# A four-layer graph network on one core: the order of the first loads, and what the planner believes of chains and of the wire

## The chip, the cores and the metric

The kernel runs on one core of a Trainium2 chip. The metric is the time of one execution on the device, in microseconds; several runs are taken, and the median is given. Five engines matter: PE (TensorE, matmuls), with PEld for its weight loads; DVE (VectorE); ACT (ScalarE); POOL (GpSimd); and SP (SyncE), which issues most of the DMAs. DMAs can also be issued from ACT and POOL.

## What is computed

32 graphs of 512 nodes with 256 features each, x of shape (32, 512, 256), and an adjacency of 512 x 512 whole numbers for every graph. Four layers follow each other, each with its own kind of attention, and each adds its result to x. All is in float32.

```python
h = relu(layernorm(x))                                 # before every layer
# layer 0
q = h @ att_W;  s = softmax(q @ h.T / 16 + where(adj == 1, 0, -1000))
y = h
for W, b in ((W0, b0), (W1, b1)):  y = tanh(s @ (y @ W + b))
x = x + y
# layer 1
Wh = h @ W.T;  e = leaky(Wh @ a1 + (Wh @ a2).T)
x = x + softmax(where(adj > 0, e, -9e15)) @ Wh
# layer 2
Hh = h @ W;    e = where(adj != 0, exp(-leaky(Hh @ a_src + (Hh @ a_dst).T)), 0)
x = x + elu((e @ Hh) / rowsum(e))
# layer 3
hW = h @ W
e = leaky((hW @ a_1).T + hW @ a_2 + hW @ a_12 @ hW.T)
p = softmax(where(adj > 0, e, -9e15))
x = x + elu(h @ W_1 + (p @ h) @ W_2)
```

## The kernel before

**Tiles.** The 512 nodes of a graph are four tiles of 128 (NT), the 256 features two halves of 128 (HC). Most products are made in two halves each way with seven products in place of eight (the helper `seven`, with sums of halves on DVE from `block_sums`); graph 0's layer 0, and the attention of layers 0, 1 and 2 in every graph and of layer 3 in the last five, are made plainly. PSUM's 8 banks, 34 pages of SBUF and a few smaller buffers are pools.

**A plan for the whole program.** No loop runs at the time of execution. Every piece of work of all 32 graphs is first noted as an operation: its engine (PE, V for DVE, A for ACT, G for POOL, D for SP's DMAs, L for a landing that no engine carries out), its cost as a pair (how long it holds the engine, when its result is there), the operations that it comes after, the buffers that it uses, and for a DMA its size in bytes. `Plan.order` then runs through time as a list scheduler: whenever an engine is free, it takes the ready operation that is due first, where the due times are counted backwards from a start time for each graph. `Plan.replay` goes through such an order and gives the time that the planner believes it will take. `Plan.best` tries start times (regular distances of 32 to 62 us and four last distances, then single graphs moved by 8, 4 and 2 us) and keeps the order that `replay` finds shortest. The kernel emits the instructions in this order; each engine then runs its own in that sequence and waits on semaphores where a result or a buffer isn't there yet. So a belief of the planner changes no instruction, but it changes the sequence on every engine, which buffer each takes, and how graphs overlap.

**What the planner believes of time.** In `order`, an operation that comes after another is ready PASS = 200 ns after the other's result, also when both are on the same engine; in `replay` it is HOP = 100 ns. A PE operation's cost has 170 ns between holding the engine and the result, so in `order` the next step of a chain on PE is ready 370 ns after PE is free of the step before. Chains on PE are: the four steps of `attend` (L794 to 796), the four of the second convolution's first product (L1049), and the four transposes of `turn` (L772). All DMAs share one wire, RATE = 200 bytes per ns, and land LAND = 2000 ns after their last byte (and 800 ns more in `order`). `SLACK` lengthens DVE's and ACT's costs by 3% in `order`.

**Before the plan's order** the constants are set, and ACT issues the load of b0 (L456), which only the values of layer 0 read (L960 for graph 0, L983 for the others).

**The start within the plan.** ACT issues two early loads (L461): layer 3's W (`l3_here`) and a12 (`a12_here`), then an activation that brings the table of functions in (`warm`, L483). W is turned on PE (L396), copied by ACT (L384), and multiplied with a12 and with itself (L414) into the matrix m3 that layer 3 needs. SP issues the four tiles of graph 0's x (L531), the weights w0 and att of layer 0 (L453), the four adjacency tiles of graph 0 (L534), and so on; in the planner w0 and att come after graph 0's x, and graph 0's adjacency after w0 and att. Graph 1's x comes after nothing. The other weights are loaded by POOL (L362), after graph 0's adjacency. A graph's x is one load of 512 KB, graph 0's is four of 128 KB. A graph's adjacency is four loads of 256 KB.

**Work of a graph that is named later.** L590 to L603: statistics, root, offset and normed rows of a layer (DVE, POOL, DVE, ACT). L608, L611, L623: the rows split in two planes of 16 bits, turned by a DMA transpose and joined again into hT. L552, L555: the adjacency as a code of 16 bits, and turned (by PE for graph 0, L559). L907: features for layers 0 and 3 (bank_f0p, bank_f3p). L933: values (bank_v, bank_w). L998 and L1166: scores of layers 0 and 3. L756, L761: a row of layers 1 and 2 sent to all partitions by way of DRAM. L791: `attend`. L868: the same by seven products, layer 3 of the first 27 graphs. L1042, L1060: second convolution of layer 0. L1247 to L1290: the end of layer 3 and the store.

Of the kernel before, what the change touches and what calls it, by code (L numbers as in the profile page):

```python
# [15 lines left out]
AF = mybir.ActivationFunctionType  # L16
# [40 lines left out]
class Plan:  # L57
# [9 lines left out]

    APART, APART_LAST = [1000.0 * k for k in range(32, 64, 2)], [1000.0 * k for k in (2, 5, 8, 12)]
    STEPS = [8000.0, 4000.0, 2000.0]
    HOP = 100.0  # L70
    LAND, RATE = 2000.0, 200.0
    SLACK = {"V": (1.03, 0.0), "A": (1.03, 0.0), "G": (1.5, 0.0), "D": (1.0, 800.0)}

    def __init__(self):
# [2 lines left out]
    def op(self, engine, cost, after, emit, graph, uses=(), size=0):  # L77


        much, more = self.SLACK.get(engine, (1.0, 0.0))  # L80
        plain, cost = cost, (cost[0] * much, cost[1] * much + more)
        flat = []
        for a in after:
            flat += a if isinstance(a, tuple) else [a]
        o = {"engine": engine, "cost": cost, "after": [a for a in flat if a is not None], "emit": emit,
             "graph": graph, "uses": list(uses), "number": len(self.ops), "size": size, "late": more, "plain": plain}
        self.ops.append(o)
        return o

# [38 lines left out]
    def replay(self, order):  # L128

        if len(order) < len(self.ops):  # L130
            return float("inf")
        at, end, owners, before, wire = {}, {}, {}, {}, 0.0
        for o in order:
            start = max([at.get(o["engine"], 0.0)] + [end[a["number"]] + self.HOP for a in o["after"]])
            for p in o["uses"]:
                where = p["pool"], p["number"]
                owner = owners.get(where)
                if owner is None or owner[0] is not p:
                    before[where] = owner[1] if owner else []
                    owner = owners[where] = p, []  # L140
                waits = before[where]
                if p["pool"] == "bank":
                    waits = waits + [x for x in owner[1] if x["engine"] != o["engine"]]
                start = max([start] + [end[x["number"]] + self.HOP for x in waits])
                owner[1].append(o)
            holds, until = o["plain"]
            if o["size"]:
                wire = max(wire, start) + o["size"] / self.RATE
                until = wire - start + self.LAND
            at[o["engine"]], end[o["number"]] = start + holds, start + until  # L150
        return max(end.values())

    def order(self, pools, starts):
        free = {pool: list(range(n)) for pool, n in pools.items()}
        users = {}
# [26 lines left out]
        while True:  # L182
            for e in engines:
                skipped = []
                while at[e] <= now and ready[e]:
# [8 lines left out]
                        p["number"] = free[p["pool"]].pop(0)  # L194
                    holds, until = o["cost"]
                    if o["size"]:
                        wire = max(wire, now) + o["size"] / self.RATE
                        until = wire - now + self.LAND + o["late"]
                    at[e] = now + holds
                    for p in o["uses"]:  # L200
                        p["ends"][e] = now + until + self.PASS
                    out.append(o)
                    heapq.heappush(events, (at[e], next(numbers), None))
                    heapq.heappush(events, (now + until + self.PASS, next(numbers), o))
                for x in skipped:
                    heapq.heappush(ready[e], x)
            if not events:
                break
            now = events[0][0]
            while events and events[0][0] <= now:  # L210
                o = heapq.heappop(events)[2]
                if o is None:
                    continue
                for p in o["uses"]:
                    p["users"] -= 1
                    if not p["users"]:
                        free[p["pool"]].append(p["number"])
                for w in users.get(o["number"], []):
                    w["left"] -= 1
                    if not w["left"]:  # L220
                        heapq.heappush(ready[w["engine"]], (w["rank"], w))
# [4 lines left out]
def kernel(  # L226
# [225 lines left out]
    for n, dst, w, key in (("w0", w0_s, w0, "raw9"), ("att", att_s, att_w, "raw10")):  # L452
        ready[key] = [prepare("D", D_X, [], lambda w=w, key=key: nc.sync.dma_start(  # L453
            out=raw(key)(), in_=rows_of(w)), key, size=P * HC * H * 4)]
        ready[n] = seven_of(raw(key), dst, HALF, ready[key], key)
    nc.scalar.dma_start(out=b0_sb, in_=line_of(b0))  # L456
    warm = const.tile([P, 1], F32, tag="warm", name="warm")

    def early(dst, src, key):
# [20 lines left out]
    ready["l2"] = seven_of(l2_wide, l2_aug, HALF + 1, a, "raw12")  # L480

    l3_here, a12_here = early(l3_sb, rows_of(l3_w), "raw2"), early(a12_sb, rows_of(l3_a12), "raw3")
    prepare("A", A_WARM, [l3_here[0], a12_here[0]], lambda: nc.scalar.activation(warm, zero, AF.Exp))  # L483
    t = transposed(l3_sb, wt3, [l3_here[1]], "raw2", "raw4", by="A")
    a = product(lambda d: awt()[:, d, :], a12_sb, lambda c: wt3()[:, c, :], H,
                t + [a12_here[1]], "raw3", "raw4", "raw5", by="A")
# [21 lines left out]
    def graph(b, adj_before, x_before, codes_before):  # L508
# [24 lines left out]
        def fetch_adj(t):  # L533
# [2 lines left out]

        got_x = [op("D", D_X, [x_before, codes_before], partial(fetch_x, ts), "x", "ahead", size=P * H * 4 * (ts.stop - ts.start))
                 for ts in ([slice(t, t + 1) for t in range(NT)] if b == 0 else [slice(0, NT)])]
        got_adj = [adj_before]
        for t in range(NT):  # L540

            got_adj.append(op("D", D_ADJ, got_adj[-1:] if b else [], partial(fetch_adj, t), "adj", size=P * N * 4))
        if b == 0:
            for n in ("raw9", "raw10"):
                ready[n][0]["after"] += got_x[-1:]
            for o in got_adj[1:]:
                o["after"] += ready["raw9"] + ready["raw10"]
            for o in loads:
                o["after"] += got_adj[-1:]

        def classes(g):
            nc.vector.tensor_scalar(T["code"][:, two(g), :], T["adj"][:, two(g), :], HUGE, None, ALU.mult)  # L552
# [740 lines left out]
            op("G", G_STORE, last, store, "y3", "slot", "ahead", size=N * H * 4)  # L1293
        return code, got_x[-1]

    codes, got_x = [None, None], [None, None]
    for b in range(B):
        code, got = graph(b, codes[-1], got_x[-2], codes[-2])
        codes.append(code)
# [38 lines left out]
```

## Time and profile before

| what | value |
|---|---|
| median of 3 runs | 2325.57 us (2325.55 to 2326.66) |
| the profiled execution | 2327.81 us, its span 2326.0 us |
| instructions | 38151 |
| first matmul / last matmul ends | 7.24 us / about 2320.2 us |
| DMA packets | 430243, 178.30 MB |
| granted clock of TensorE, mean | 0.999 |

The page has the busy time of each engine, the span in 40 slices, the chain of work that ended last, and the costliest groups of instructions. PE is where the chain runs: it has 92% of it, ACT 3%, DVE 2%, DMA 1%. The largest group on it:

```profile
L791 PE MATMUL bank_a<-v,e 128*128 128x258 f32 (+2 forms) x3232 | 817.2, 381 | 1.3 <-DVE e L1080 0.6
```

A line of this kind gives the source line, engine, operation, what is written from what, shapes and count, then the busy time in us and the mean of one in ns, then the idle time of the engine ahead of it and what ended most of that. Matmuls overlap in these records (a mean of 381 ns, while they start some 217 ns apart), so the distance from one start to the next tells more than the length of one.

### The profile page before, as it was taken

Reading aid. Unit: us, or ns where it says so; the run is one execution under the profiler, and the core shown is the slowest. Engines: PE = TensorE matmul, PEld = TensorE weight load, DVE = VectorE, ACT = ScalarE, POOL = GpSimd, SP = SyncE. Lnnn points to the kernel's source line nnn. Section 1 sums busy time; section 2 is a strip of 40 time slices with the busy share of each in tenths; the row PEclk is TensorE's granted clock in tenths of the full one; section 3 lists DMA queues with packets and bytes.
Section 4 is the critical chain, followed back from the end, with each engine's and each line's share of the span. In section 5 each row is a group of like instructions: output and inputs, shape, how many; then the busy total and the mean of one; then the engine's idle time right before and its main releaser. Section 6 shows DMA issues by size and latency. Waiting matters only on the chain.

```text
span 2326.0 us, 38151 instructions
## 1 busy us (share of the span) xinstructions
PE 2307.2 (99%) x13022; PEld 1996.3 (86%) x13022; DVE 2113.0 (91%) x5310; ACT 1720.1 (74%) x3279; POOL 257.5 (11%) x341
## 2 busy tenths in 40 slices
PE   8999999999999999999999999999999999999998
PEld 6888888888888888888888888988888888888887
DVE  6888889999999999999999999999999999998998
ACT  4677778767787777787777877778867778666884
POOL 2101101110101010100101011101111011010110
PEclk9999999999999999999999999999999999999999
DMA  6441233423333323333233333233332333321221
GB/s 163 114 96 37 60 78 78 91 61 74 89 73 87 73 69 87 87 73 82 66 79 87 76 87 70 70 88 83 75 82 63 87 82 73 92 54 25 61 50 45
DMA packets 430243, 178.30 MB, mean 77 GB/s; under 512 B 384128, under 2 KB 402176, under 8 KB 430048
## 3 DMA queue, kind: packets, MB, share of 16 engines
q1 hardware_dynamic: 424288, 157.51, 31.3%
q0 software_dynamic: 5072, 17.70, 2.3%
q8 instruction: 102, 1.67, 0.3%
q14 instruction: 93, 0.76, 0.1%
q10 hardware_dynamic: 688, 0.66, 0.1%
HBM read 67.64 MB, written 16.89 MB: 36 GB/s over the span
## 4 chain that ended last, share of the span: by engine, by line
PE 92%; ACT 3%; DVE 2%; DMA 1%; issue 0%; SPq 0%; ACTq 0%; DVEq 0%
PE bank_a L791 28%; PE bank_z L1042 8%; PE bank_s3p L1166 5%; PE bank_q0p L998 5%; PE bank_o L1060 4%; PE bank_v0p L933 4%; PE bank_f0p L907 4%; PE bank_w3p L933 4%; PE bank_f3p L907 4%; PE bank_a3p L868 4%; PE bank_s3q L1166 3%; PE bank_q0q L998 3%; PE bank_a3q L868 3%; PE bank_v1p L933 2%; PE bank_v2p L933 2%; PE bank_v3p L933 2%
## 5 line engine op out<-in xcount | busy, mean ns | idle before, releaser
L791 PE MATMUL bank_a<-v,e 128*128 128x258 f32 (+2 forms) x3232 | 817.2, 381 | 1.3 <-DVE e L1080 0.6
L791 PEld LDWEIGHTS bank_a<-v,e 128*128 128x128 f32 x3232 | 576.4, 190 | 70.6 <-issue 5.2
L603 ACT ACTIVATE xn<-x,off,rstd 128x256 f32<-128x256 f32 x512 | 278.2, 598 | 203.0 <-DVE off L599 197.6
L596 POOL TENSOR_TENSOR rstd<-ve,mhalf 128x2 f32<-128x2 f32 x256 | 222.4, 899 | 1737.6 <-DVE ve L593 1537.6
L623 ACT COPY hT<-planesT 128x512 uint16<-128x512 uint16 x508 | 375.9, 771 | 47.4 <-DMA planesT<-planes 47.0
L1042 PE MATMUL bank_z<-e,y 128*128 128x512 f32 x512 | 240.5, 593 | 0.0
L590 DVE BATCH_NORM_STATS2 st<-x 128x6 f32<-128x512 f32 x256 | 177.3, 698 | 9.3 <-DMA x<-in_x_dram 8.0
L608 DVE COPY planes<-xn 128x512 uint16<-128x512 uint16 x380 | 155.4, 419 | 13.6 <-DMA planesT<-planes 8.2
L765 ACT ACTIVATE e<-row,v 128x512 f32<-128x512 f32 x224 | 154.7, 727 | 5.2 <-DMA row<-row 5.2
L1042 PEld LDWEIGHTS bank_z<-e,y 128*128 128x128 f32 x512 | 90.6, 191 | 64.4 <-issue 59.5
L768 ACT ACTIVATE e<-e 128x1024 f32<-128x1024 f32 x128 | 136.8, 1069 | 0.1
L1060 PE MATMUL bank_o<-w_sb,zT 128*128 128x256 f32 x512 | 117.4, 379 | 0.0
L1173 DVE SCALAR_TENSOR_TENSOR e<-bank_s3p,v,mask 128x256 f32<-128x256 f32 x256 | 111.4, 477 | 3.7 <-PE bank_s3p L1166 3.2
L1006 ACT ACTIVATE e<-e 128x512 f32<-128x512 f32 x124 | 77.9, 634 | 43.6 <-DVE e L1017 41.8
L1060 PEld LDWEIGHTS bank_o<-w_sb,zT 128*128 128x128 f32 x512 | 96.9, 190 | 13.0
L697 DVE TENSOR_TENSOR hs<-hT,hs 128x256 f32<-128x256 f32 x254 | 105.9, 417 | 0.4
L728 ACT COPY v<-bank_v2p 128x258 f32<-128x258 f32 x128 | 48.2, 377 | 70.1 <-PE bank_v2p L933 69.0
L700 DVE TENSOR_TENSOR hs<-hT 128x512 f32<-128x512 f32 x127 | 86.9, 684 | 11.7 <-ACT hT L623 11.3
L1080 DVE SCALAR_TENSOR_TENSOR e<-codeT,e 128x1024 f32<-128x1024 bf16 x64 | 78.0, 1219 | 12.5 <-ACT e L768 12.4
L1009 DVE TENSOR_TENSOR e<-bank_q0p,mask 128x512 f32<-128x512 f32 x124 | 84.8, 684 | 4.0 <-PE bank_q0p L998 3.4
L1261 ACT ACTIVATE r<-y,one 128x512 f32<-128x512 f32 (+1 forms) x65 | 46.5, 715 | 50.8 <-DVE y L1271 42.8
L1111 DVE SCALAR_TENSOR_TENSOR e<-codeT,e 128x1024 f32<-128x1024 bf16 x64 | 77.9, 1218 | 6.6 <-ACT e L768 6.5
(224 smaller groups left out, 5386.9 us busy)
## 6 DMA issues: line engine op xcount, KB each, us to landing
adj<-in_adj_dram SPq DMA_DIRECT2D x128, 256.0 KB
x<-in_x_dram SPq DMA_DIRECT2D x31, 512.0 KB
out_dram<-y POOLq DMA_DIRECT2D x31, 512.0 KB, 3.4
row<-row SPq DMA_DIRECT2D x56, 256.0 KB
planesT<-planes SPq DMA_TRANSPOSE x508
codeT<-code SPq DMA_TRANSPOSE x124
crest<-crest SPq DMA_TRANSPOSE x64
row<-sT SPq DMA_DIRECT2D x56, 2.0 KB
```

The lines of the kernel that those rows point to most:

```text
L590: nc.vector.bn_stats(T[f"st{l}"][:, g, :], T["x"][:, two(g), :].rearrange("p t h -> p h t"))
L596: nc.gpsimd.tensor_tensor(T[f"rstd{l}"][:, two(g)], T[f"ve{l}"][:, two(g)], mhalf[:, two(g)], ALU.pow)
L603: nc.scalar.activation(T[f"xn{l}"][:, t, :], T["x"][:, t, :], AF.Relu, bias=T[f"off{l}"][:, t : t + 1], scale=T[f"rstd{l}"][:, t : t + 1])
L623: nc.scalar.copy(bits[:, :, :, t * P : (t + 1) * P], T[f"planesT{l}_{t}"].rearrange("p (b c) n -> p b c n", b=2))
L791: nc.tensor.matmul(T[key][:, : LEAD + H + 1 - lead], e(l, c)[:, t * P : (t + 1) * P], T[f"v{l}"][:, c, lead:], start=(c == 0), stop=(c == ...
L868: nc.tensor.matmul(p[:, i * WIDE : i * WIDE + k], a[:, j, i * P : (i + 1) * P], b_[:, j, :], start=fresh and i == j == 0, stop=True, skip_ ...
L907: nc.tensor.matmul(p[:, : N // 2], w[:, x - 1, :], right(x), start=fresh, stop=True, skip_group_check=True)
L933: nc.tensor.matmul(p[:, j * k : (j + 1) * k], right(x)[:, j * P : (j + 1) * P], w[:, x - 1, :], start=fresh and j == 0, stop=True, skip_gr ...
L998: nc.tensor.matmul(p[:, j * N // 2 : (j + 1) * N // 2], right(x)[:, j * P : (j + 1) * P], left(x), start=fresh and j == 0, stop=True, skip ...
L1042: nc.tensor.matmul(T[f"bank_z{k}"], T["y0"][:, c, k * P : (k + 1) * P], e(0, c), start=(c == 0), stop=(c == NT - 1))
L1060: nc.tensor.matmul(T[key][:, j * H : (j + 1) * H], T["zT"][:, k, t * P : (t + 1) * P], w1_sb[:, k, :], start=(k == 0), stop=(k == HC - 1))
L1166: nc.tensor.matmul(p[:, j * N // 2 : (j + 1) * N // 2], left(x)[:, j * P : (j + 1) * P], right(x), start=fresh and j == 0, stop=True, skip ...
```

## The change

Six edits, in two groups.

1. Loads. b0's load is no longer issued before the plan's order. It becomes an operation of ACT behind a12's load, which now comes after W's load; the table's activation comes after b0's issue. Graph 1's x comes after all four adjacency loads of graph 0 (`first_adj`).
2. The planner's beliefs. A new function `way` gives the time from a result to an operation that comes after it. Across engines it stays as it was (100 ns in `replay`, 200 in `order`). On the same engine it becomes: for PE, the negative of the 170 ns, so that the next step of a chain is ready as soon as PE is free; for DVE and ACT SELF = 40 ns. The wire's rate becomes 300 bytes per ns for plain DMAs and 190 for operations with the cost D_TURN, the DMA transposes (`on_wire`). In `order`, buffers are still given back PASS after the end, but the operations that come after are now woken each at its own time.

No instruction is added or taken away in the work itself; costs of operations stay as they are.

```diff
@@ -67,8 +67,8 @@
 
     APART, APART_LAST = [1000.0 * k for k in range(32, 64, 2)], [1000.0 * k for k in (2, 5, 8, 12)]
     STEPS = [8000.0, 4000.0, 2000.0]
-    HOP = 100.0
-    LAND, RATE = 2000.0, 200.0
+    HOP, SELF = 100.0, 40.0
+    LAND, RATE, TURN_RATE = 2000.0, 300.0, 190.0
     SLACK = {"V": (1.03, 0.0), "A": (1.03, 0.0), "G": (1.5, 0.0), "D": (1.0, 800.0)}
 
     def __init__(self):
@@ -83,7 +83,7 @@
         for a in after:
             flat += a if isinstance(a, tuple) else [a]
         o = {"engine": engine, "cost": cost, "after": [a for a in flat if a is not None], "emit": emit,
-             "graph": graph, "uses": list(uses), "number": len(self.ops), "size": size, "late": more, "plain": plain}
+             "graph": graph, "uses": list(uses), "number": len(self.ops), "size": size, "late": more, "plain": plain, "turns": plain is D_TURN}
         self.ops.append(o)
         return o
 
@@ -131,7 +131,7 @@
             return float("inf")
         at, end, owners, before, wire = {}, {}, {}, {}, 0.0
         for o in order:
-            start = max([at.get(o["engine"], 0.0)] + [end[a["number"]] + self.HOP for a in o["after"]])
+            start = max([at.get(o["engine"], 0.0)] + [end[a["number"]] + self.way(a, o, self.HOP) for a in o["after"]])
             for p in o["uses"]:
                 where = p["pool"], p["number"]
                 owner = owners.get(where)
@@ -145,10 +145,20 @@
                 owner[1].append(o)
             holds, until = o["plain"]
             if o["size"]:
-                wire = max(wire, start) + o["size"] / self.RATE
+                wire = max(wire, start) + self.on_wire(o)
                 until = wire - start + self.LAND
             at[o["engine"]], end[o["number"]] = start + holds, start + until
         return max(end.values())
+
+    def on_wire(self, o):
+
+        return o["size"] / (self.TURN_RATE if o["turns"] else self.RATE)
+
+    def way(self, a, o, other):
+
+        if a["engine"] != o["engine"] or o["engine"] not in ("PE", "V", "A"):
+            return other
+        return a["plain"][0] - a["plain"][1] if o["engine"] == "PE" else self.SELF
 
     def order(self, pools, starts):
         free = {pool: list(range(n)) for pool, n in pools.items()}
@@ -194,28 +204,28 @@
                         p["number"] = free[p["pool"]].pop(0)
                     holds, until = o["cost"]
                     if o["size"]:
-                        wire = max(wire, now) + o["size"] / self.RATE
+                        wire = max(wire, now) + self.on_wire(o)
                         until = wire - now + self.LAND + o["late"]
                     at[e] = now + holds
                     for p in o["uses"]:
                         p["ends"][e] = now + until + self.PASS
                     out.append(o)
-                    heapq.heappush(events, (at[e], next(numbers), None))
-                    heapq.heappush(events, (now + until + self.PASS, next(numbers), o))
+                    heapq.heappush(events, (at[e], next(numbers), None, None))
+                    heapq.heappush(events, (now + until + self.PASS, next(numbers), o, None))
+                    for w in users.get(o["number"], []):
+                        heapq.heappush(events, (now + until + self.way(o, w, self.PASS), next(numbers), None, w))
                 for x in skipped:
                     heapq.heappush(ready[e], x)
             if not events:
                 break
             now = events[0][0]
             while events and events[0][0] <= now:
-                o = heapq.heappop(events)[2]
-                if o is None:
-                    continue
-                for p in o["uses"]:
+                _, _, o, w = heapq.heappop(events)
+                for p in o["uses"] if o else ():
                     p["users"] -= 1
                     if not p["users"]:
                         free[p["pool"]].append(p["number"])
-                for w in users.get(o["number"], []):
+                if w:
                     w["left"] -= 1
                     if not w["left"]:
                         heapq.heappush(ready[w["engine"]], (w["rank"], w))
@@ -453,7 +463,6 @@
         ready[key] = [prepare("D", D_X, [], lambda w=w, key=key: nc.sync.dma_start(
             out=raw(key)(), in_=rows_of(w)), key, size=P * HC * H * 4)]
         ready[n] = seven_of(raw(key), dst, HALF, ready[key], key)
-    nc.scalar.dma_start(out=b0_sb, in_=line_of(b0))
     warm = const.tile([P, 1], F32, tag="warm", name="warm")
 
     def early(dst, src, key):
@@ -480,7 +489,9 @@
     ready["l2"] = seven_of(l2_wide, l2_aug, HALF + 1, a, "raw12")
 
     l3_here, a12_here = early(l3_sb, rows_of(l3_w), "raw2"), early(a12_sb, rows_of(l3_a12), "raw3")
-    prepare("A", A_WARM, [l3_here[0], a12_here[0]], lambda: nc.scalar.activation(warm, zero, AF.Exp))
+    a12_here[0]["after"].append(l3_here[0])
+    b0_here = prepare("A", A_ISSUE, [a12_here[0]], lambda: nc.scalar.dma_start(out=b0_sb, in_=line_of(b0)))
+    prepare("A", A_WARM, [b0_here], lambda: nc.scalar.activation(warm, zero, AF.Exp))
     t = transposed(l3_sb, wt3, [l3_here[1]], "raw2", "raw4", by="A")
     a = product(lambda d: awt()[:, d, :], a12_sb, lambda c: wt3()[:, c, :], H,
                 t + [a12_here[1]], "raw3", "raw4", "raw5", by="A")
@@ -536,6 +547,8 @@
 
         got_x = [op("D", D_X, [x_before, codes_before], partial(fetch_x, ts), "x", "ahead", size=P * H * 4 * (ts.stop - ts.start))
                  for ts in ([slice(t, t + 1) for t in range(NT)] if b == 0 else [slice(0, NT)])]
+        if b == 1:
+            got_x[0]["after"] += first_adj
         got_adj = [adj_before]
         for t in range(NT):
 
@@ -547,6 +560,7 @@
                 o["after"] += ready["raw9"] + ready["raw10"]
             for o in loads:
                 o["after"] += got_adj[-1:]
+            first_adj.append(got_adj[-1])
 
         def classes(g):
             nc.vector.tensor_scalar(T["code"][:, two(g), :], T["adj"][:, two(g), :], HUGE, None, ALU.mult)
@@ -1293,7 +1307,7 @@
             op("G", G_STORE, last, store, "y3", "slot", "ahead", size=N * H * 4)
         return code, got_x[-1]
 
-    codes, got_x = [None, None], [None, None]
+    codes, got_x, first_adj = [None, None], [None, None], []
     for b in range(B):
         code, got = graph(b, codes[-1], got_x[-2], codes[-2])
         codes.append(code)
```

## The prediction

> **What bounds the kernel now.** I read the page's busy table and slices first, then the chain of waits, then stages by window, then the first microseconds in the timeline, then SP's own waits.
>
> ```profile
> PE 2307.2 (99%) x13022; PEld 1996.3 (86%) x13022; DVE 2113.0 (91%) x5310; ACT 1720.1 (74%) x3279; POOL 257.5 (11%) x341
> ...
> PE   8999999999999999999999999999999999999998
> ```
>
> PE is busy from end to end. So the change can win only where PE waits, and can lose wherever it makes PE wait more. The chain of waits in order of time says the same for the middle of the run; each line is the second convolution of one graph (L1060):
>
> ```profile
> 885.31 3.45 PE bank_o L1060 x16
> 956.52 3.45 PE bank_o L1060 x16
> 1028.50 3.45 PE bank_o L1060 x16
> 1099.71 3.45 PE bank_o L1060 x16
> ```
>
> The distance is 71.21 us, 71.98 once, then 71.21 again up to 1598.18. Stages by window tell whether the 71.21 have a hole (the columns: stage, its length, then busy and count of PE, PEld, DVE, ACT, POOL):
>
> ```profile
> 600.00:1000.00 400.00, 400.00 (x2301) 350.80 (x2300) 374.20 (x932) 299.17 (x574) 40.33 (x55) 1.00 0.35 78
> 1000.00:1100.00 100.00, 99.50 (x566) 84.82 (x566) 92.88 (x232) 78.07 (x150) 10.75 (x15) 1.00 0.40 77
> 1100.00:1600.00 500.00, 500.00 (x2865) 436.29 (x2864) 466.95 (x1164) 379.19 (x724) 51.05 (x70) 1.00 0.35 79
> 1600.00:2000.00 400.00, 398.79 (x2291) 348.40 (x2290) 369.73 (x925) 295.03 (x566) 48.75 (x57) 1.00 0.36 79
> 2200.00:2320.00 120.00, 117.76 (x671) 104.50 (x669) 112.95 (x271) 84.39 (x155) 9.41 (x10) 1.00 0.20 44
> ```
>
> They have none: a graph in the regular part costs 71.21 us of PE work, and no reordering makes that shorter. The idle column understates a stall, since a matmul's modelled end covers the start of the gap: the hole at 1000 to 1100 shows 0.50 us, but the period grew by 0.77. So I took the matmul records in order of start and subtracted from each distance the usual one of its shape (0.216 us at 256 columns, 0.218 at 258, 0.112 at 128, 0.430 at 512). What exceeds it by more than 15 ns sums to about 15.6 us at 80 places: 4.4 in the first 100 us (2.2 of it L414 at half pace before 12.7), then 0.2 to 300, 1.8 to 600, 0.8 around 1027, 2.5 from 1600 to 2000, 1.6 to 2200 and 4.2 to the end: 11.1 us after the first 100. Outside lie 7.24 us before the first matmul and about 5.8 after the last (2320.2 to 2326.0). That is all there is to win.
>
> The first microseconds:
>
> ```profile
> 0.74 0.40 ACTq L456 DMA_DIRECT2D b_sb<-in_L_gnn_b_dram  x1
> 0.74 2.41 SPq L531 DMA_DIRECT2D x<-in_x_dram  x5
> ...
> 1.17 0.47 ACTq L461 DMA_DIRECT2D raw_w<-in_L_gnn_W_dram  x1
> 1.67 0.49 ACTq L461 DMA_DIRECT2D raw_w<-in_L_gnn_a_dram  x1
> ...
> 5.98 0.38 SPq L453 DMA_DIRECT2D raw_w<-in_L_gnn_W_dram  x1
> ...
> 7.24 1.08 PE L396 MATMUL bank_w<-ident,raw_w 128*128 128x128 f32 x4 [7.24 <-DMA raw_w<-in_L_gnn_W_dram]
> ```
>
> PE begins when layer 3's W is there, issued second on ACT's queue, landed at 7.10. Five loads of x are the four tiles of graph 0 and the whole of graph 1 (512 KB). SP then stands still from 3.15 to 5.98:
>
> ```profile
> SPq L453 <- DMA b_sb<-in_L_gnn_b_dram: 2.8, 1, 2.8
> ```
>
> The ninth DMA of the program reuses the completion semaphore of the first, b0's, and waits for it.
>
> **What the Trainium skill says.** "DMA: Bandwidth & Descriptors", section "Queues, rings and completion order": SP's and ACT's queues run on the same 16 engines, and completion does not follow the order of issue. The trace agrees: W, issued at 1.17, needs 5.93 us while x is in flight, and the engines are 0.91 to 1.10 busy from 4 to 12 us. "TensorE: Matmul & The Clock Gate", section "What's actually happening": a cold PE runs at half clock until a free-running window has been busy. Here L414 starts every 0.43 us until about 12.7 and every 0.216 later. The same page, "Step-by-step: what each phase is for": matmuls keep program order, only weight loads are pulled ahead; so a chain on PE needs no pause, and here 20 matmuls of L791 take 4.35 us, 0.2175 each. "VectorE: DVE Perf Modes", section "The DRAIN you can't avoid": chained operations cost the same with or without a semaphore between. Here L434 (12.50, 0.28 long) is followed by its reader L435 at 12.82, 0.04 us after its end, which is the change's SELF.
>
> **Part 1: W first, a12 second, b0 third.** No instruction is added; b0's issue (0.40) moves from before the manual order to behind two issues on ACT, before the activation that warms the table. W goes out at 0.74, so 0.43 us earlier. b0's 128 KB leave the queue ahead of it: at the 297 to 367 GB/s of 4 to 8 us at most 0.4 us, at least nothing if x is what W shares the wire with. So W lands 0.43 to 0.83 earlier; I take 0.65. Queued behind on ACT is only the table load, at 2.19 as before. b0's reader (L960) runs at 16.47; b0 issued near 1.7 lands with a12, before 8.3. While PE is cold, an earlier start is worth half if the clock rises at the same moment: 0.2 to 0.8 us for the end, and I take 0.6. Is x late then? The first transposes of xn (13.17) follow ACT's xn at 12.44, which could have started after the offset at 10.34 to 10.50 but stood behind the copy of the product at 12.17: 1.9 us of room. After 13.3 the chain is PE alone up to 53, so the gain passes on.
>
> **Part 2: graph 1's x behind graph 0's adjacency.** One 0.53 us issue leaves SP's first five, past w0, att and four adjacency issues. The first eight DMAs are then W, a12, b0, four x and w0, so w0 no longer waits for b0 and leaves near 2.6 instead of 5.98; att becomes the ninth and waits for W. w0 and att are read on DVE at 11.76 and 14.54, and the adjacency, landed by 14.0, at 17.83: they only gain cover, 0 us. Graph 1's x lands near 14 instead of 10.0 (the bytes in total are the same and their last one lands at 14.0 today). Its statistics move from 10.42 to about 14.1. Its first PE instruction is L907 at 32.97, with the last join of hT done at 28.8: 4.2 us of room for a delay of about 4. Cost 0, up to +0.5 if DVE's full stretch at 14 to 20 us must absorb it.
>
> **Part 3: the planner.** The work stays the same; only the order on each engine, the buffer numbers and the graphs' start times change. Before, order() makes the next step of a PE chain wait 170 + 200 ns after the one before, and replay() 170 + 100. On the chip this pause doesn't exist. So the plan holds fictitious PE idle time or foreign work pushed into it, PE arrives earlier than planned, and meets ACT or DVE not ready. Near L791 the records show about 3.6 us in nine places after 100 us (526.1: 0.72; 2307.3: 0.71; 2003.7: 0.47; 2244.2: 0.42). The rest, 7.5 us, is mostly ACT's or DVE's copies and sums before f3p, a3p, v2p, behind transposes and row loads that came late (1810.6: 1.05; 2247.9: 0.87; 1026.9: 0.67); own rates on the wire (300 and 190 instead of 200) address these in part. The model can't make the rest of the order worse than its replay knows, but DVE and ACT lose the 160 ns that every dependent pair had as reserve. Bounds: all 11.1 gone; or as much again added, because nothing in this trace fixes the new order. I take half gone, 5.5 us: what is late next is DVE, at 93.5% (374.20 of 400). The tail after the last matmul is the same DVE, ACT and DMA sequence: 0.
>
> **Sum.** -0.6 - 5.5 = -6.1 us. The profiled execution took 2327.81 us for a span of 2326.0; it would be 2321.7. The median of the runs is 2.24 lower: 2325.57 - 6.1 = 2319.5, 0.26% less. I call 0.2% (4.65 us) what a measurement of this kernel can tell from no change.
>
> **Rivals.** *Same order quality, 0.31.* The new order stalls as much as the old in other places; only the start is won, with 4 us of scatter: 2325.0, from 2321 to 2330. For it: the plan is a greedy search, and the regular part is already free of holes, so better modelling has only the edges to mend. Against it: the model now matches what the trace shows of chains.
>
> *A hole in every period, 0.25, slower.* The regular part repeats one order some 20 times. With 160 ns less reserve per dependent pair, one place in it, such as ACT's copy of bank_f3p before the next product or DVE's sums before it, becomes late, and is so in each graph. One hole of the size seen at 1027 (0.5 to 0.77 us) costs 20 x 0.5 = 10 us; with the start's 0.6 and some 2 at the edges won back, 2325.57 - 2.6 + 10 = 2333. It decides from 0.13 us per graph on (2.6 / 20) and passes 0.2% at 0.36. For it: DVE has only 4.6 us free in 71.21. Against it: PE's work per period is unchanged and DVE's is still below it.
>
> *W is hidden anyway.* If W lands no earlier, 0.6 is lost: 2320.1, no case of its own.
>
> **How the numbers follow.** Faster by over 0.2%: 0.44, the forecast with 2314 to 2320.9. Within 0.2%: 0.31. Slower: 0.25. The low end 2314 is the start's 0.8 and nine tenths of the 11.1; the high end 2332 takes in holes of up to 0.45 us per period. Its own range for the likeliest case is 2314 to 2321.
>
> **What would show it.** Part 1: first matmul at 6.4 to 6.8, W's load first on ACT. Part 2: SP's fifth issue is w0, with no stop at 3.15; statistics of graph 1 after 13. Part 3: L791 four steps in a row more often (the chain's pieces x16 and longer), PE idle in the windows from 300 on falling from 5.4 us to about half. It is wrong if L1060 stands more than 71.3 us apart in the regular part, or if the windows from 1600 on still hold 4 us of idle.

## The result and the profile after

The changed kernel takes 2322.36 us in the median of 22 runs (2319.89 to 2324.31), the kernel before 2325.88 us in 22 runs beside it (2324.43 to 2327.25). The ratio is 0.9983, with a 95% interval of 0.9977 to 0.9989: 0.17% faster, -3.5 us. The forecast was -6.1 us (2319.5), with 0.44 on faster by over 0.2%; the measured 0.17% lies in the class within 0.2%, which had 0.31.

The profiled execution took 2323.26 us for a span of 2320.7; the span is 5.3 us shorter than before's. The profiled execution of before lay 1.9 us above its own median, that of the change 0.9 above, and executions of one kernel differ by 2 to 5 us. So some 1 to 2 of the 5.3 us are chance of these two executions, and the traces are used to say where time goes, the medians to say how much.

The page of the changed kernel, busy times:

```profile
PE 2307.0 (99%) x13022; PEld 1999.2 (86%) x13022; DVE 2113.4 (91%) x5310; ACT 1714.6 (74%) x3279; POOL 268.6 (12%) x341
```

PE has the same work and is as busy; only what lies around it is less. Its timeline at the start (start, length, engine, line, operation):

```profile
0.74 0.47 ACTq L470 DMA_DIRECT2D raw_w<-in_L_gnn_W_dram  x1
...
0.74 1.81 SPq L542 DMA_DIRECT2D x<-in_x_dram  x4
...
1.24 0.49 ACTq L470 DMA_DIRECT2D raw_w<-in_L_gnn_a_dram  x1
...
1.75 0.49 ACTq L493 DMA_DIRECT2D b_sb<-in_L_gnn_b_dram  x1
...
2.60 0.43 SPq L463 DMA_DIRECT2D raw_w<-in_L_gnn_W_dram  x1
...
4.50 1.09 PE L406 MATMUL bank_w<-ident,raw_w 128*128 128x128 f32 x4 [4.50 <-DMA raw_w<-in_L_gnn_W_dram]
```

PE begins at 4.50 instead of 7.24. W needs 3.6 us from issue to landing (0.74 to 4.37) where it needed 5.93. SP has no stop after its fourth load; it stands once, from 3.03 to 4.38, until W has landed, and then issues att. The stages by window (length, then busy and count of PE, PEld, DVE, ACT, POOL; then clock, DMA share, GB/s):

```profile
600.00:1000.00 400.00, 399.86 (x2303) 350.42 (x2302) 373.98 (x934) 296.54 (x574) 44.40 (x56) 1.00 0.34 77
...
1100.00:1600.00 500.00, 499.44 (x2861) 435.38 (x2860) 465.38 (x1163) 375.74 (x725) 56.79 (x70) 1.00 0.35 78
1600.00:2000.00 400.00, 399.86 (x2301) 350.19 (x2300) 372.17 (x939) 293.71 (x564) 47.19 (x57) 1.00 0.36 80
2000.00:2200.00 200.00, 198.01 (x1111) 170.53 (x1111) 172.61 (x434) 155.38 (x297) 23.44 (x26) 1.00 0.24 51
```

The middle is nearly without holes, as before. The stage 1600 to 2000 lost its holes (1.21 us idle to 0.14); 2000 to 2200 has more than before (0.61 to 1.99). The very end is shorter too. Of before, then of the change, the chain of waits in order of time (start, length, what), from the reciprocal that ends the wait for the last product:

```profile
2321.51 0.09 DVE rs L1247
2321.59 0.02 issue
2321.62 0.50 DVE y L1252
2322.11 0.02 issue
2322.14 0.52 ACT r L1261
2322.66 0.02 issue
2322.68 0.43 DVE y L1264
```

```profile
2311.91 3.96 PE bank_a L805 x18
2315.86 0.02 issue
2315.89 0.03 DVE rs L1261
...
2317.36 0.42 DVE y L1278
```

Before, PE's last matmul began at 2319.90, and the chain comes to this reciprocal 1.6 us later, since DVE was still at the tiles before. Now the last matmul began at 2315.47 and the reciprocal follows it within 0.4 us.

Adding up the two traces, with waits of PE taken as in the prediction (what a matmul starts later than its shape needs, where that is over 15 ns):

| piece | before | after | difference |
|---|---|---|---|
| up to the first matmul | 7.24 | 4.50 | -2.73 |
| PE's waits up to 100 us | 4.4 | 5.6 | +1.2 |
| PE's waits after 100 us | 11.2 | 8.4 | -2.9 |
| from the last matmul's start to the end | 6.15 | 5.24 | -0.91 |

These are -5.3 together, the difference of the spans. In the third row chance is large: three runs below that keep the order of before (e1, e2, e3) have 10.1, 9.3 and 10.0 us there, two that keep the order of the change (e7, e9) 7.8 and 8.0.

### The profile page after: what moved, and what is told of

Its sections match the earlier page's. It is cut to its first block, busy times and chain, and to the rows that moved or that the text cites. A ratio compares the mean times of both kernels' runs of the same rounds, so it can differ in the third digit from the quotient of the medians.

```text
span 2320.7 us, 38152 instructions
## 1 busy us (share of the span) xinstructions
PE 2307.0 (99%) x13022; PEld 1999.2 (86%) x13022; DVE 2113.4 (91%) x5310; ACT 1714.6 (74%) x3279; POOL 268.6 (12%) x341
## 4 chain that ended last, share of the span: by engine, by line
PE 95%; DVE 2%; ACT 2%; DMA 1%; issue 0%; DVEq 0%
PE bank_a L805 29%; PE bank_z L1056 9%; PE bank_s3p L1180 5%; PE bank_o L1074 5%; PE bank_q0p L1012 4%; PE bank_w3p L947 4%; PE bank_f0p L921 4%; PE bank_v0p L947 4%; PE bank_a3p L882 4%; PE bank_f3p L921 4%; PE bank_s3q L1180 4%; PE bank_q0q L1012 3%; PE bank_a3q L882 3%; PE bank_v3p L947 2%; PE bank_v1p L947 2%; PE bank_v2p L947 2%
## 5 line engine op out<-in xcount | busy, mean ns | idle before, releaser
L805 PE MATMUL bank_a<-v,e 128*128 128x258 f32 (+2 forms) x3232 | 801.0, 381 | 1.0 <-DVE e L1125 0.8
L610 POOL TENSOR_TENSOR rstd<-ve,mhalf 128x2 f32<-128x2 f32 x256 | 233.5, 932 | 1785.7 <-DVE ve L607 1688.6
L637 ACT COPY hT<-planesT 128x512 uint16<-128x512 uint16 x508 | 381.5, 772 | 64.1 <-DMA planesT<-planes 55.9
L1226 ACT ACTIVATE e<-e,zero 128x1024 f32<-128x1024 f32 x64 | 73.2, 1149 | 28.0 <-DVE crest L1204 22.9
L1229 DVE TENSOR_TENSOR e<-e,crest 128x1024 f32<-128x1024 f32 x64 | 76.9, 1218 | 8.5 <-ACT crest L1223 8.3
```

The costliest lines, as they stand in the source:

```text
L610: nc.gpsimd.tensor_tensor(T[f"rstd{l}"][:, two(g)], T[f"ve{l}"][:, two(g)], mhalf[:, two(g)], ALU.pow)
L637: nc.scalar.copy(bits[:, :, :, t * P : (t + 1) * P], T[f"planesT{l}_{t}"].rearrange("p (b c) n -> p b c n", b=2))
L805: nc.tensor.matmul(T[key][:, : LEAD + H + 1 - lead], e(l, c)[:, t * P : (t + 1) * P], T[f"v{l}"][:, c, lead:], start=(c == 0), stop=(c == ...
```

## The experiments

All medians are of 13 to 21 runs beside the kernel before on the same chip, except where noted. "Order kept" means that the sequence of the named kernel stays as it is on every engine and only the named loads are issued elsewhere. The last four columns are us of the profiled execution, with waits of PE as above.

| run | median us | ratio to before, 95% interval | first matmul | waits to 100 us | waits after | last matmul to end |
|---|---|---|---|---|---|---|
| change (22 runs) | 2322.36 | 0.9983 (0.9977 to 0.9989) | 4.50 | 5.6 | 8.4 | 5.2 |
| e1_w_first | 2323.82 | 0.9991 (0.9983 to 0.9999) | 4.44 | 5.6 | 10.1 | 6.1 |
| e2_x1_late | 2327.18 | 1.0006 (0.9997 to 1.0014) | 7.21 | 5.7 | 9.3 | 6.1 |
| e3_both_loads | 2326.74 | 1.0005 (0.9997 to 1.0013) | 4.32 | 9.0 | 10.0 | 6.1 |
| e4_plan_only | 2324.08 | 0.9993 (0.9985 to 1.0001) | 7.21 | 4.2 | 9.5 | 5.2 |
| e5_chains_only | 2325.96 | 0.9999 (0.9991 to 1.0007) | 4.51 | 7.5 | 8.2 | 6.1 |
| e6_rates_only | 2326.23 | 0.9999 (0.9991 to 1.0007) | 4.60 | 6.7 | 10.1 | 6.7 |
| e7_b0_first | 2324.13 | 0.9994 (0.9986 to 1.0002) | 7.38 | 4.6 | 7.8 | 5.3 |
| e8_x1_free | 2323.68 | 0.9991 (0.9984 to 0.9997) | 4.42 | 5.7 | 9.4 | 5.3 |
| e9_x1_early | 2325.02 | 0.9994 (0.9986 to 1.0002) | 4.45 | 7.4 | 8.0 | 5.2 |
| e10_rate_250 | 2323.19 | 0.9987 (0.9980 to 0.9993) | 4.34 | 5.5 | 8.1 | 6.2 |
| e11_finer_steps | 2321.76 | 0.9983 (0.9976 to 0.9991) | 4.34 | 5.7 | 6.4 | 5.3 |
| e12_row_by_pe | 2326.25 | 1.0001 (0.9993 to 1.0009) | 4.30 | 4.9 | 12.0 | 5.5 |

### b0 alone, both ways

The kernel before, order kept:

```diff
-    nc.scalar.dma_start(out=b0_sb, in_=line_of(b0))
+        def issue():
+            nc.scalar.dma_start(out=dst(), in_=src)
+            if key == "raw3":
+                nc.scalar.dma_start(out=b0_sb, in_=line_of(b0))
```

> The order of the kernel before is kept instruction for instruction on every engine; only b0's load is issued by ACT right behind a12's load instead of ahead of W's. Theory Q (the queue: b0's 128 KB lay ahead of W on ACT's own queue): first matmul at 4.4 to 5.0 us instead of 7.24, and the end 2.0 to 2.7 us earlier (2323.2 to 2323.9). Theory X (the wire: W came late because graph 1's 512 KB of x ran beside it): W gains only its 0.43 us of issue and a little more, first matmul at 6.4 to 6.8, end 0.3 to 0.8 us earlier.

The mirror, the changed kernel with its order kept and b0 issued first again:

```diff
+    nc.scalar.dma_start(out=b0_sb, in_=line_of(b0))
-    b0_here = prepare("A", A_ISSUE, [a12_here[0]], lambda: nc.scalar.dma_start(out=b0_sb, in_=line_of(b0)))
+    b0_here = prepare("A", A_ISSUE, [a12_here[0]], lambda: None)
```

> The changed kernel with its order kept instruction for instruction, but b0's load issued by ACT ahead of W again. The mirror of the run that moved b0 alone: first matmul at 7.2 instead of 4.50 and 2.0 to 2.7 us later at the end (2324.4 to 2325.1) if the queue theory holds in this order too; less than 1 us later if this order had another hold-up behind the first matmul.

Theory Q holds for PE's start in both: moving b0 takes it from 7.24 to 4.44, putting it back from 4.50 to 7.38. The end moves by -2.3 us one way and +1.8 the other, a little less than the 2.0 to 2.7 expected; the interval of the second run just overlaps that of the change. A third pair stands among the runs below: e4 (b0 first) and e8 (b0 third) have the same sequence on every engine apart from ACT's first three issues. There PE's start moves from 7.21 to 4.42 as well, but the median only by 0.4 us, and by 0.1 if each is taken against the kernel before beside it. The trace of e8 shows a wait that took part of the gain:

```profile
9.02 1.30 DVE L602 BATCH_NORM_STATS2 st<-x 128x6 f32<-128x512 f32 x2 [0.53 <-DMA x<-in_x_dram]
...
11.20 0.44 PE L628 MATMUL bank_n<-ident,xn 128*128 128x128 f32 x2 [1.18 <-ACT xn L615]
```

In that order the statistics of graph 1 stand on DVE ahead of graph 0's first offset, so PE waits for graph 0's normed rows. An earlier start of PE is therefore worth 0.1 to 2.3 us at the end, by the order behind it.

The landings in the records say more than the theory did. With b0 first, even x's first tile, which is on SP's queue and was issued at the same moment, landed at 5.76; with W first, at 3.60, and W at 4.31 instead of 7.10. Nor was the wire full. The stages by window of before, then of the run with W first (its last numbers are DMA share and GB/s):

```profile
2.00:4.00 2.00, 0.00 (x0) 0.00 (x0) 0.00 (x0) 1.49 (x2) 0.00 (x0) 1.00 0.51 139
```

```profile
2.00:4.00 2.00, 0.00 (x0) 0.00 (x0) 0.00 (x0) 1.49 (x2) 0.00 (x0) 1.00 0.85 259
```

So it isn't b0's 128 KB as bytes: while b0 is ahead, 139 GB/s pass on all queues together, without it 259. b0's load has one row of 1 KB in DRAM as the source of all 128 partitions; it took 5.2 us to land. The dip follows b0: where b0 is third, 129 (e1), 207 (e3), 223 (e9) and 260 GB/s (the change) pass from 5 to 6 us, and 353 in before. So b0's load holds back what runs beside it. Whether that comes from reading one row 128 times no run varied, and it stays open: in the kernel before, the 56 loads of a row to all partitions (L761, 256 KB from one row of 2 KB) landed after 3.5 us in the median, and the 128 adjacency loads of the same size after 3.0, a smaller difference.

### Graph 1's x

The kernel before with w0, att and graph 0's adjacency pulled ahead of graph 1's x, order kept otherwise; and the same with b0 behind a12:

```diff
     order, took = plan.best(POOLS)
+    last_adj, x1 = moved
+    first = order.index(x1)
+    ahead = [o for o in order[first:order.index(last_adj) + 1] if o["engine"] == "D" and o is not x1]
+    order = order[:first] + ahead + [o for o in order[first:] if o not in ahead]
```

> The order of the kernel before is kept, except that w0, att and the four adjacency loads of graph 0 are issued ahead of graph 1's x; b0 stays ahead of W. Theory Q: first matmul at 7.0 to 7.3, end within 0.3 us of before. Theory X: first matmul at 5.0 to 6.0, end 1 to 2 us earlier.

> Both moves of loads, the order of the kernel before kept otherwise. First matmul at 4.5 under either theory. If an earlier start passes to the end undiminished: 2.7 us less, 2323.2. If graph 0's x or the cold clock holds PE up next: 1.0 to 1.8 us less. The rest up to the 3.5 us of the whole change is then the plan's: 0.8 or about 2.

Theory X falls (first matmul at 7.21), but e2 ends 1.1 us later than before, and e3 is 2.9 us worse than e1, which neither theory said. In the trace SP issues x between the second and the third adjacency tile, so these two runs do most, not all, of the second part. The timeline of DVE in e3 shows what they add:

```profile
9.25 0.16 DVE L606 SCALAR_TENSOR_TENSOR off<-st,rstd 128x2 f32<-128x2 f32 x1 [0.64 <-POOL rstd L603]
12.26 1.30 DVE L597 BATCH_NORM_STATS2 st<-x 128x6 f32<-128x512 f32 x2 [2.85 <-DMA x<-in_x_dram]
13.48 0.15 DVE L606 SCALAR_TENSOR_TENSOR off<-st,rstd 128x2 f32<-128x2 f32 x1
```

In the old order graph 1's statistics stand on DVE between the two offsets of graph 0. Once its x is late, graph 0's second offset waits behind them (11.23 in e1, 13.48 here), and PE waits 2.6 us for the normed rows; the half clock that followed in this execution cost some 1.8 more. So this test was not one of the wire: a load can be moved back only together with the instructions that stand behind its reader. Two more runs do that. In e8 the planner orders anew without the second part; in e9 the changed kernel keeps its order, and only the issue of graph 1's x is put back ahead of w0.

```diff
-        if b == 1:
-            got_x[0]["after"] += first_adj
```

> The change without its second part: graph 1's x comes after nothing again, and the planner orders anew. Moving b0 alone gave -2.3 us and the plan alone -2.0, their sum is -4.3, the whole change -3.5. If graph 1's x behind the adjacency costs the 0.8: this is at 2321.6. If it is needed (graph 1's 512 KB hold up graph 0's weights and adjacency): 0.5 to 2 us later than the changed kernel. If it is indifferent: within 0.5 us of 2322.4.

```diff
     order, took = plan.best(POOLS)
+    w0_here, x1 = ready["raw9"][0], moved[0]
+    order = [o for o in order if o is not x1]
+    order.insert([o is w0_here for o in order].index(True), x1)
```

> The changed kernel with its order kept on every engine, but graph 1's x is issued behind graph 0's x again, ahead of w0, att and the adjacency. Its reader on DVE stays where the change has it (16.6 us), so nothing of graph 0 can stand behind it there. If the second part buys wire time for graph 0's weights and adjacency: they land 1 to 2 us later, PE waits for w0 or att between 12 and 16 us, and the end is 0.5 to 2 us later. If it buys nothing by itself and matters only through the order that the planner makes: within 0.5 us of the changed kernel (2322.4).

Without the second part the kernel is 1.3 us later in the medians when ordered anew, and 2.7 us later with the order kept (the intervals of both overlap that of the change, so the sizes are rough). The place is not PE's wait for w0 or att, as I expected, but DVE again. The timeline of DVE with x early, then in the change:

```profile
8.36 0.29 DVE L608 TENSOR_SCALAR ve<-st 128x2 f32<-128x2 f32 x2
9.93 0.29 DVE L440 COPY w_s<-raw_w 128x256 f32<-128x256 f32 x1 [1.27 <-DMA raw_w<-in_L_gnn_W_dram]
...
11.34 0.22 DVE L614 SCALAR_TENSOR_TENSOR off<-st,rstd 128x2 f32<-128x2 f32 x2
```

```profile
7.59 0.29 DVE L607 TENSOR_SCALAR ve<-st 128x2 f32<-128x2 f32 x2
7.79 0.29 DVE L440 COPY w_s<-raw_w 128x256 f32<-128x256 f32 x1
...
9.19 0.37 DVE L613 SCALAR_TENSOR_TENSOR off<-st,rstd 128x2 f32<-128x2 f32 x2
```

w0 lands at 7.61 in the change and at 9.90 here; its sums stand on DVE ahead of graph 0's offsets; the normed rows begin at 11.57 instead of 9.71, and PE waits 1.4 us. In the order of the change the second part is thus worth some 2.7 us, of which PE's waits up to 100 us show 1.8. The 1.3 of e8 are those of another order too: its trace loses after 100 us (9.4 against 8.4), not before (5.7 against 5.6).

### The planner's beliefs

The kernel before with the change's planner (`way`, `on_wire` and the numbers below) and neither part of the loads; the change with one rate of 200; and the change with the old waits inside engines:

```diff
-    HOP = 100.0
-    LAND, RATE = 2000.0, 200.0
+    HOP, SELF = 100.0, 40.0
+    LAND, RATE, TURN_RATE = 2000.0, 300.0, 190.0
```

```diff
-    LAND, RATE, TURN_RATE = 2000.0, 300.0, 190.0
+    LAND, RATE, TURN_RATE = 2000.0, 200.0, 200.0
```

```diff
-        if a["engine"] != o["engine"] or o["engine"] not in ("PE", "V", "A"):
-            return other
-        return a["plain"][0] - a["plain"][1] if o["engine"] == "PE" else self.SELF
+        return other
```

> The planner's new beliefs alone; b0 first and graph 1's x free as before. If the plan itself saves what the trace of the changed kernel shows after 100 us (stalls of 8.5 us there instead of 11.1): 2 to 3 us less, 2323 to 2324. If the loads did all of it: within 1 us of before. If the new beliefs do harm without graph 1's x bound behind the adjacency: slower by 1 to 5 us.

> The changed kernel with the wire's rate back at 200 for every DMA; loads and the rule for chains as in the change. If the chain rule carries the plan's gain (my step: 3.6 of 11.1 us of stalls lay beside attend), this equals the changed kernel within 1 us, 2321.5 to 2323.5. If the rates carry it: 2 us later, about 2324.5.

> The changed kernel with the old waits inside PE, DVE and ACT (100 and 200 ns for everything); loads and rates as in the change. If the chain rule carries the gain: about 2324 to 2325, and a matmul's hole near attend again. If the rates do: within 1 us of the changed kernel.

Alone, the planner gives -2.0 us (its interval just reaches 1). With b0 moved it gives nothing more: e8, with the planner and b0, ends at 2323.68, and e1, with b0 alone, at 2323.82. So the -2.3 of b0 and the -2.0 of the planner don't add; together they come to -2.2, and only with graph 1's x behind the adjacency to -3.5. No run has both moves of loads ordered anew by the old planner, so what the new beliefs add to them isn't measured. And either belief without the other, with the better loads, is no faster than before: the 2.3 us that the loads bring are given back. The run with chains alone waits 7.5 us in the first 100 and ends later, that with rates alone has 10.1 us after 100 and the longest end. Neither expectation held: the gain isn't that of chains nor that of rates, nor a sum of two. What the traces do show is that after 100 us the order of the change is better than that of before, whichever of these loads go with it: PE's waits after 100 us are 7.8 to 8.4 us in the change, e7 and e9, and 9.3 to 11.2 in before, e1, e2 and e3, and from the last matmul's start to the end they take 5.2 to 5.3 us against 6.1 to 6.2.

Is the pair better, or is it one lucky order? Two shifts around it:

```diff
-    LAND, RATE, TURN_RATE = 2000.0, 300.0, 190.0
+    LAND, RATE, TURN_RATE = 2000.0, 250.0, 190.0
```

> The change with plain DMAs at 250 instead of 300 bytes per ns in the planner, all else as in the change. If the pair of beliefs is better in a lasting way, a small shift of one keeps the gain: 2321.5 to 2323.5. If the gain is the luck of one order among many: anything from 2321 to 2327, as the two single beliefs gave (2325.96 and 2326.23).

```diff
-    STEPS = [8000.0, 4000.0, 2000.0]
+    STEPS = [8000.0, 4000.0, 2000.0, 1000.0, 500.0]
```

> The change with two finer steps (1 and 0.5 us) in the planner's search of start times, all else as in the change. If what the planner believes carries over to the chip, an order that it holds for shorter is shorter: 1 to 2 us less than the changed kernel, 2320.5 to 2321.5. If differences of a few us between its orders are not seen by it: within 2 us of 2322.4 on either side.

Both keep the gain (0.9987 and 0.9983). The first has another order from 14 us on and other holes (2.6 us in 400 to 500) of the same sum. The second keeps the change's order on PE up to 1595 us and changes only what follows, so it is no full repeat; its median is 0.6 us lower, too little to tell. The last run below also has both beliefs and both moves of loads, with an order that is another from 64 us on and 8 small transposes more, and it is no faster than before (2326.25). So two shifts kept the gain and one lost it: luck of the order is not excluded.

### Two waits near 2196 us, and the clock

The change waits 1.2 and 1.0 us at 2195.4 and 2197.0, for ACT's copy of bank_f3p and for DVE's masked weights. The run with finer steps has the same two waits at 2194.8 and 2196.4. Stages by window of the change, then of the run with finer steps (the clock is the third number from the end):

```profile
2195.00:2199.00 4.00, 2.12 (x12) 1.43 (x11) 4.00 (x9) 4.00 (x8) 0.00 (x0) 0.96 0.12 24
2199.00:2202.00 3.00, 3.00 (x10) 2.46 (x9) 1.07 (x3) 1.71 (x3) 0.00 (x0) 0.50 0.37 63
```

```profile
2195.00:2199.00 4.00, 2.12 (x9) 1.54 (x9) 3.44 (x7) 4.00 (x8) 0.00 (x0) 1.00 0.18 37
2199.00:2202.00 3.00, 3.00 (x21) 2.76 (x21) 2.84 (x5) 2.97 (x7) 0.00 (x0) 1.00 0.32 44
```

PE is busy all the 3 us in both, but does 10 matmuls in one and 21 in the other: in the change the clock fell to half at 2198.68 for 3.41 us. The last experiment aimed at these waits. It turns the rows of layers 1 and 2 of graph 29 on PE, as the last two graphs have it:

```diff
-            turned = b < TURNED or b >= B - TURNED
+            turned = b < TURNED or b >= B - TURNED - 1
```

> The run with finer steps, and graph 29's rows of layers 1 and 2 turned on PE (as the last two graphs have them) instead of sent by way of DRAM; 8 more transposes on PE, some 0.9 us. Theory R: the two gaps near 2196 (1.2 and 1.0 us, in the changed kernel followed by a stretch at half clock) come from the late row: written at 2184.3, spread at 2189.2 behind two transposes on SP, on hand at 2193.4, after which ACT and DVE are late for the products. Then no gap of over 1 us is left between 2180 and 2210, no half clock in the profile, and the end is 1 to 2 us before the run with finer steps (2319.8 to 2320.8). Rival: DVE and ACT are short of time there whatever the row does; then gaps of the same sum come nearby, and the 0.9 us of PE's work is lost: 2321.5 to 2324.

Theory R falls, and the rival took too little: 2326.25, 4.5 us behind the run with finer steps. The two waits are gone, but with the planner's new order, another from 64 us on, one of 3.1 us has come, and half clock behind it. So the row was not varied alone. The timeline of PE:

```profile
2184.87 1.92 PE L805 MATMUL bank_a<-v,e 128*128 128x259 f32 x8
2189.74 4.57 PE L805 MATMUL bank_a<-v,e 128*128 128x258 f32 x12 [2.95 <-DVE e L1125]
```

What holds DVE's masked weights up there, the row apart, stays open. No version was found that is clearly faster than the change.

## Why the prediction was right, and where it wasn't

The direction was right and the time lies in the whole range (2314 to 2332), but at 2322.36 it lies outside the 2314 to 2321 of the likeliest case and in the class within 0.2%. That -6.1 came as near to -3.5 as it did is in part luck: the terms for the loads were too small, the term for the planner too large, and as the runs show they don't add. (The low end was rounded down: 2325.57 - 0.8 - 10.0 is 2314.8.)

**Part 1, W first: mis-sized.** The step "b0's 128 KB leave the queue ahead of it: at the 297 to 367 GB/s ... at most 0.4 us" took b0 for bytes on a full wire. W landed 2.73 us earlier, not 0.65; the end moved by 2.3 in the run of b0 alone, not 0.6, though by 1.8 in the order of the change and 0.1 to 0.4 in that of e8. The step "so the gain passes on" held only in part. The row for this stood in the trace: x's first 128 KB, issued at 0.74 with nothing ahead on their own queue, landed only at 5.76, while the wire was half used. The halving for the cold clock was partly right: PE's waits in the first 100 us grew by 1.2 us in the change and in the run of b0 alone. In the change that is in part the half clock, which lasted to 10.74: 12 distances between L424 instructions were too long, 2.6 us in sum, 10 and 2.2 before. In the run of b0 alone it is not (10 distances, 2.0 us); there PE waits 0.7 us for graph 0's normed rows at 10.79. For these rows the prediction had counted 1.9 us of room, less than the 2.8 us by which PE came earlier.

**Part 2, graph 1's x: wrong.** Forecast 0, at worst a loss of 0.5; it gains some 2.7 us in the order of the change, and in the old order it lost (e3 against e1, 2.9 us). The step "w0 and att ... only gain cover, 0 us" looked at when PE reads them. What counted was DVE's queue, where the sums of w0 stand ahead of graph 0's offsets. That SP's fifth issue would be w0 and graph 1's statistics fall after 13 us was right (2.60; 16.57), and so was att's wait for W (issued at 4.38, W landed at 4.37).

**Part 3, the planner: too much.** Forecast half of 11.1 us, 5.5. The step "I take half gone" was mis-sized: in the trace the waits after 100 us fell by 2.9 (2.1 in the mean over all traces of the two orders), with 1.7 us of the half clock near 2200 counted against it, and the end shortened by 0.9, which the forecast had put at 0. The runs of the planner alone gave 2.0. The argument by chains did not hold by itself: chains alone give nothing.

**The rivals.** The hole in every period did not come: 400 us of the regular part hold 0.14 us of idle, 500 us hold 0.56. The second convolutions no longer stand at one distance there: from 600 to 1590 us it goes from 70.3 to 72.2 us, past the 71.3 named as a sign of being wrong, but its mean is 71.3 as before. Equal order quality, with only the start won, was nearer in size (2325.0 forecast, if the start is put at 0.6; with the measured 2.3 it would have been 2325.57 - 2.3 = 2323.3) but not in kind: the order gained too, though not in e8 against e1. Its range, 2321 to 2330, holds the measured time.

The first matmul came at 4.50, outside the 6.4 to 6.8 named as a sign; PE's idle time in the windows from 300 on went from 5.4 to 3.4 us, short of half. Pieces of 16 and more matmuls of `attend` in a row went from 10 to 15, as foreseen.

## What to carry to other kernels

Look for the landing time of every early load, on all queues, and compare it with its bytes: here one slow load held back loads on another queue. When a load is moved, follow the queue of the engine that reads it, not only the critical engine: everything behind that reader in program order inherits its lateness, so load and order have to be changed together. With a planner at 99% of its bound engine, try beliefs together and repeat with small shifts before crediting a belief: here four orders made with both beliefs and both moves of loads, three of them with a small shift, ended from 2321.8 to 2326.3.

## What the runs showed of the hardware

A load of 128 KB whose source is one row of 1 KB for all partitions took 5.2 us from issue to landing, and with it ahead a plain load on another queue landed at 5.76 instead of 3.60. With W first it was issued third, at 1.75 in the change, and took 4.8 us.

Eight completion semaphores serve the early DMAs in turn: the ninth stood on SP until the first had landed, at 5.98 in before (b0 landed at 5.96) and at 4.38 in the change (W landed at 4.37).

PE's clock fell to half for 3.41 us after waits of 1.2 and 1.0 us close together (the change; also e8 and e9), of 2.6 us (e3) and of 3.1 us (e12), and did not after the same pair of waits in e4, e7 and e11. In each of the 14 profiles the moments at which the clock changed lie whole multiples of 3.413 us apart (in the change 10.74, 2198.68 and 2202.09: 641 and 1). Cut at these multiples, the five stretches ahead of a fall hold 2.3 to 2.4 us of PE's waits (the change, e8, e9), 2.8 (e3) and 3.1 (e12); in e4, e7 and e11 the pair is divided differently, and no stretch there holds more than 2.1. So the place of the waits in such a stretch fits as what decides. The Trainium skill's page "TensorE: Matmul & The Clock Gate", section "What's actually happening", fits in part: its window of some 3.4 us that runs freely agrees with the length and the multiples; that the clock falls after a whole idle window is more than was needed here, where PE worked in between. What such a fall costs is about half its length: in the change the distances between 2198.5 and 2202 were too long by 1.7 us in all.

The full clock came 4.3 us after the first matmul in e1, 5.5 in the kernel before and 6.2 in the change, from 3.5 (e2) to 6.2 over all profiles. In all 14 it came at the end of the first such stretch that began after the first matmul (in the change 7.32 to 10.74, the first matmul at 4.50).
